# Two places instead of six for the value products of layer 1's attention, in a two-layer kernel on one core

## The chip, the cores and the metric

The kernel runs on one core of a Trainium2 chip. The engines of that core work side by side and each takes its own instructions in order: TensorE (PE, matrix products), VectorE (DVE), ScalarE (ACT), GpSimd (POOL) and SyncE (SP, which issues DMAs). The metric is the device time of one execution in microseconds (us); lower is better. Three executions before the change took 1373.52, 1379.36 and 1386.26 us; their median is 1379.36 us.

## The reference

The program is two transformer layers over x of shape (2, 1024, 256). Each adds an attention part and a feed-forward part to x, both taken from the same layer norm. The change touches only the attention of layer 1, which has 16 heads and one shared latent (64 values per token) for keys and values:

```
scores = (einsum('bhsc,btc->bhst', q_abs, kv) + einsum('bhsd,bxtd->bhst', q_pe, k_pe)) * SCALE
scores = where(causal, scores, finfo.min)
attn = softmax(scores, axis=-1)
x = einsum('bhst,btc->bhsc', attn, kv)
x = einsum('bhsc,hdc->bhsd', x, out_absorb)
return x.transpose(0, 2, 1, 3).reshape(b, s, NH * VH) @ wo.T
```

The third einsum, weights times latent, is the "value product" of the title.

## The kernel before

Layer 0 and the preparation of layer 1 (feed-forward, layer norm, latent, joined weights) come first and end some 712 us into the execution. What follows is layer 1's attention, which ends the program.

**How it is tiled.** The queries are cut into blocks of 128 tokens: two batch entries b, and in each the blocks i = 7 down to 0, the longest first. A block is worked in two halves of eight heads (g = 0, 1). One half of a block is a *step*: 32 steps, and two more turns of the loop that only drain. Block i sees the first w = 128 (i + 1) keys because of the causal mask, so a head has two score products where i is 4 or more (512 keys, and the remaining 512, 384, 256 or 128), and one where i is 3 or less.

**One head's path.** `scores` (L1165) multiplies queries with keys on PE into a PSUM bank of the tag "s", of which there are two (the pool has `bufs=2`). L1179 on DVE reads that bank, adds the mask, writes the result to SBUF as `p` and carries a running minimum `nmax` from a head's first bank to its second; the bank is then free for the next score product. L1186 on ACT takes the exponential of the whole row and its sum. Two heads later `turn_over` (L1190) on DVE transposes `p` in 32x32 blocks into `pT`. When all eight heads of a step are there, `product` (L1212) multiplies `pT` with the latent `vrep`: the call `product(s, sb)` takes 32 keys out of each quarter and issues eight small matmuls (32 rows by 64 columns of the array each, 128 columns of data), accumulated over sb = 0 .. nsb - 1 with nsb = 4 (i + 1) in the four banks `ps_o`. The profile counts two PE records for each fp32 matmul, so one sb is 16 records.

**What sets the order.** The stage is under a manual schedule: the order of the Python calls is the order on each engine. The loop at L1266 goes through the steps; in each there are nine *places*, h = 0 to 8, and at place h it issues, in this order: the score products of head h (none at place 8), then what was put on `late[h]` (work for DVE, ACT and POOL), then what was put on `side[h]` (work for PE), then one `turn_over` of the head two before. What is put where:

- `side[0]`: the rotary part of the queries of the next block (`project("pe")`, L1122, 16 records); `late[1]`: the previous step's reciprocal (`inverse`, L1193) and the rotation (`rotate`, on DVE, ACT and POOL).
- `side[1]`, only in steps with g = 1: the output projection of the block before (`output`, L1241, 16 records).
- `side[2]`: the latent part of the queries of the next block (`project("lat")`, L1122, 16 records), and behind it the first value products.
- `side[2]` to `side[7]`: the value products of the previous step.
- `side[7]`, last: `inverse_T` (L1203), which turns the reciprocals on PE (L1206, 4 records); ACT copies them (L1210), and `late[8]`, `normalize` (L1224), multiplies `ps_o` with them on DVE.

The line that deals the value products to places is the one that is changed; `prev` is the step before, and n its nsb:

```
n = prev.nsb
for sb in range(n):
    side[2 + 6 * sb // n].append(lambda sb=sb: product(prev, sb))
side[7].append(lambda: inverse_T(prev))
late[8].append(lambda: normalize(prev))
```

## Time and profile before

| what | value |
|---|---|
| three executions | 1373.52, 1379.36, 1386.26 us |
| the profiled execution, its own time | 1381.07 us |
| its span, first to last instruction | 1379.4 us |
| mean granted TensorE clock | 0.939 of full |
| busy over the span: PE, DVE, ACT, POOL | 1222.4, 823.1, 634.3, 559.8 us |
| share of the chain that ended last: PE, DVE, ACT | 67%, 13%, 7% |
| layer 1's attention | from 712 us to the end of the span |
| PE busy from 760 to 1320 us, by stretches of 40 us | 38.62 to 40.00 us each |
| DVE busy in the same stretches | 21.65 to 31.09 us each |

A row of the profile names the line, the engine, the operation, its tiles (out<-in), its shape and the number of records. In a timeline the first column is the start in us from the beginning of the span, the second the length, and a bracket at the end gives the engine's idle time before the row and what released it. Matmuls are pipelined and their ends are modelled, so the length of a PE row holds some time in which the next one already runs: the distance from one PE row's start to the next one's start is the better measure. `DVE_READ_ACCUMULATOR2_ANT` is the second half of L1179, which delivers `nmax`.

### The profile page before, as it was taken

How to read it: one execution, taken by the hardware profiler on the slowest of the kernel's cores; microseconds unless marked ns; L12 is line 12 of the kernel's file. 1: busy time of each engine (PE TensorE's matmuls, PEld its weight loads, DVE VectorE, ACT ScalarE, POOL GpSimd, SP SyncE). 2: the span in 40 equal slices, each digit the busy share in tenths (PEclk: the TensorE clock that was granted, in tenths of full speed). 3: DMA queues.
4: the chain of work that ended last, by engine and by line, in shares of the span. 5: the costliest groups of instructions: out<-in, count | busy, mean ns of one | idle time of the engine just before them, and what ended most of it. 6: DMA issues, size and time to landing. Idle time of an engine off the chain costs nothing.

```text
span 1379.4 us, 36540 instructions
## 1 busy us (share of the span) xinstructions
PE 1222.4 (89%) x15295; PEld 839.5 (61%) x15295; DVE 823.1 (60%) x2098; ACT 634.3 (46%) x1193; POOL 559.8 (41%) x644
## 2 busy tenths in 40 slices
PE   6778888887878886679778999999999999999998
PEld 3545555564545554557554667676775676777675
DVE  3775665655566416533307777776657777766653
ACT  2545656654455552223215434444555444444553
POOL 4575556554462431474214322323454232243340
PEclk9779999999998997779959999999999999999998
DMA  7463323322220003000340000000000000000000
GB/s 175 125 137 89 61 62 81 74 62 47 62 39 9 1 1 122 23 7 25 77 126 8 3 14 3 14 14 14 14 14 13 14 8 10 14 14 6 13 19 13
DMA packets 139044, 56.06 MB, mean 41 GB/s; under 512 B 110112, under 2 KB 136096, under 8 KB 138656
## 3 DMA queue, kind: packets, MB, share of 16 engines
q1 hardware_dynamic: 133296, 48.10, 14.5%
q10 hardware_dynamic: 4816, 3.02, 0.7%
q0 software_dynamic: 768, 2.62, 0.7%
q8 instruction: 120, 1.97, 0.6%
q14 instruction: 44, 0.36, 0.1%
HBM read 36.93 MB, written 14.68 MB: 37 GB/s over the span
## 4 chain that ended last, share of the span: by engine, by line
PE 67%; DVE 13%; ACT 7%; issue 4%; POOL 3%; DMA 3%; SPq 2%; ACTq 0%; DVEq 0%; POOLq 0%
PE ps_s L1173 19%; PE ps_o L1217 12%; PE ps_t L1122 7%; DVE masked L499 4%; PE ps_t L1241 4%; PE ps_o L574 4%; PE ps_m L679 3%; PE ps_ms L484 2%; PE ps_ms L537 2%; DVE p L1179 2%; PE ps_m L358 1%; ACT p L551 1%; PE ps_ms L543 1%; PE ps_o L1003 1%; PE ps_m L635 1%
## 5 line engine op out<-in xcount | busy, mean ns | idle before, releaser
L1186 ACT ACTIVATE p<-p,nmax 128x1024 f32<-128x1024 f32 (+7 forms) x256 | 198.4, 775 | 330.2 <-DVE nmax L1179 329.2
L1173 PE MATMUL ps_s<-kT,qc 128*128 128x512 f32 (+3 forms) x768 | 309.5, 515 | 7.5 <-DVE nmax L1179 7.0
L551 ACT ACTIVATE p<-ps_ms 128x1024 f32<-128x1024 f32 x144 | 147.3, 1026 | 168.5 <-PE ps_ms L543 167.5
L1191 DVE STREAM_TRANSPOSE pT<-p 128x1024 f32<-128x1024 f32 (+7 forms) x256 | 197.8, 773 | 0.2 <-ACT p L1186 0.2
L1173 PEld LDWEIGHTS ps_s<-kT,qc 128*128 128x128 f32 x768 | 127.3, 192 | 111.0 <-issue 65.2
L1217 PE MATMUL ps_o<-pT,vrep 32*64 32x128 f32 x9216 | 183.3, 281 | 1.9 <-DVE xT L1226 1.8
L1217 PEld LDWEIGHTS ps_o<-pT,vrep 32*64 32x64 f32 x9216 | 138.4, 131 | 71.2 <-issue 63.0
L1198 POOL COPY rb<-rinv 128x512 f32<-128x512 f32 x32 | 19.6, 612 | 377.0 <-DVE rinv L1196 349.2
L1140 POOL TENSOR_TENSOR qc<-t,t 32x512 f32<-32x512 f32 x128 | 161.9, 1265 | 8.2
L1179 DVE CUSTOM_DVE_ANT_0 p<-ps_s,zeros 128x512 f32<-128x512 f32 x128 | 87.6, 684 | 69.9 <-PE ps_s L1173 69.2
L1179 DVE CUSTOM_DVE_ANT_0 p<-ps_s,maskz 128x512 f32<-128x512 f32 (+3 forms) x128 | 62.2, 486 | 81.5 <-PE ps_s L1173 81.2
L492 DVE TENSOR_REDUCE peak<-ps_ms 128x2 f32<-128x1024 f32 x64 | 77.5, 1218 | 38.0 <-PE ps_ms L484 37.9
L559 POOL TENSOR_SCALAR_AFFINE_SELECT p<-p 128x256 f32<-128x256 f32 (+1 forms) x112 | 47.8, 442 | 113.1 <-ACT p L551 112.7
L537 PE MATMUL ps_ms<-head,head 64*128 64x512 f32 (+3 forms) x384 | 65.1, 377 | 25.1 <-DVE peak L499 22.2
L499 DVE CUSTOM_DVE_ANT_0 masked<-ps_ms,maskz,peak 128x512 f32<-128x512 f32 (+3 forms) x128 | 70.4, 550 | 27.0 <-PE ps_ms L484 22.3
L574 PE MATMUL ps_o<-p,v 128*32 128x512 f32 (+3 forms) x768 | 82.7, 520 | 0.0
L1179 DVE CUSTOM_DVE_ANT_0 p<-ps_s,maskz,nmax 128x512 f32<-128x512 f32 (+3 forms) x128 | 70.5, 551 | 20.2 <-PE ps_s L1173 3.6
L1136 POOL TENSOR_TENSOR t<-t,sinq 128x512 f32<-128x512 f32 x32 | 40.7, 1271 | 93.4 <-ACT t L1135 89.6
L484 PE MATMUL ps_ms<-head,head 64*128 64x512 f32 (+3 forms) x384 | 71.7, 417 | 7.1 <-DVE head L424 5.6
L652 POOL TENSOR_TENSOR h<-whole,h 128x512 fp32r<-128x512 f32 x32 | 41.0, 1280 | 87.4 <-ACT h L650 87.4
L499 DVE CUSTOM_DVE_ANT_0 masked<-ps_ms,maskz 128x512 f32<-128x512 f32 (+3 forms) x128 | 62.6, 489 | 12.2 <-PE ps_ms L484 6.5
L1122 PEld LDWEIGHTS ps_t<-qnT,wpe 96*128 96x128 f32 x512 | 63.2, 196 | 10.6 <-ACT t L1135 3.4
(239 smaller groups left out, 2095.5 us busy)
## 6 DMA issues: line engine op xcount, KB each, us to landing
stage<-rows SPq DMA_DIRECT2D x232, 64.0 KB, 2.8
rows<-proj SPq DMA_DIRECT2D x13, 512.0 KB, 3.3
rows<-proj SPq DMA_DIRECT2D x14, 256.0 KB, 2.6
v<-rows SPq DMA_DIRECT2D x32, 64.0 KB, 2.8
wo<-in_wo SPq DMA_DIRECT2D x8, 256.0 KB, 3.5
x<-x_sb SPq DMA_DIRECT2D x8, 256.0 KB, 3.2
xin<-x SPq DMA_DIRECT2D x16, 128.0 KB, 2.2
out<-xin SPq DMA_DIRECT2D x16, 128.0 KB, 1.7
```

The lines of the kernel that those rows point to most:

```text
L484: nc.tensor.matmul(t[:, c % 2, off + col : off + col + w], q[:, i * P : (i + 1) * P], k[:, k0 : k0 + w], start=True, stop=True, tile_posit ...
L499: nc.vector.tensor_tensor_reduce(masked[:, :w], at, maskz[:, SC - w :], -1.0, dst if k0 else 3.0e38, ALU.add, ALU.min, dst,)
L537: nc.tensor.matmul(t[:, c % 2, off + col : off + col + w], k[:, j * P : (j + 1) * P], q[:, at - w : at], start=(off + col == 0), stop=Fals ...
L551: nc.scalar.activation(p, t, AF.Exp)
L574: nc.tensor.matmul(quad(box["o"], c)[:, SC - w :], values[g % 2][:, j, c, :], p[:, c % 2, off + col : off + col + w], start=first, stop=fi ...
L1122: nc.tensor.matmul(box[key][:, r * P : (r + 1) * P], w[:, c, QP * g + r, :], qnT[:, c, tok], start=(c == 0), stop=(c == 1),)
L1140: nc.gpsimd.tensor_tensor(qc[b, i][64 + 32 * x : 96 + 32 * x, g, hh], t1[at : at + 32], t2[at : at + 32], ALU.add,)
L1173: nc.tensor.matmul(sc[:, : n1 - n0], qc[s.b, s.i][:, s.g, h // QP, h % QP, :], kT[:, s.b * S + n0 : s.b * S + n1], start=True, stop=True,)
L1179: nc.vector.tensor_tensor_reduce(s.p[:, n0:n1], sc[:, : n1 - n0], mask, -1.0, 3.0e38 if n0 == 0 else s.nmax, ALU.add, ALU.min, nmax,)
L1186: nc.scalar.activation(p[:, :w], p[:, :w], AF.Exp, bias=nmax, scale=-1.0, accum_out=rsum)
L1191: nc.vector.transpose(s.pT[:, : s.nsb, h, :], p[:, : 32 * s.nsb])
L1217: nc.tensor.matmul(s.o[64 * hh : 64 * hh + 64, c, : QP * 32], vrep[32 * c : 32 * c + 32, s.b * 32 + sb, :], s.pT[32 * c : 32 * c + 32, sb, ...
```

## The change

One line. The index of the place goes from `2 + 6 * sb // n` to `2 + 3 * (2 * sb // n)`:

```
                 if prev is not None:
                     n = prev.nsb
                     for sb in range(n):
-                        side[2 + 6 * sb // n].append(lambda sb=sb: product(prev, sb))
+                        side[2 + 3 * (2 * sb // n)].append(lambda sb=sb: product(prev, sb))
                     side[7].append(lambda: inverse_T(prev))
                     late[8].append(lambda: normalize(prev))
```

The first half of the sb go to place 2 and the second half to place 5; places 3, 4, 6 and 7 have none. For nsb = 32 that is two runs of 16 calls (128 matmuls, 256 records) where there were six runs of 5 or 6. For nsb = 4 there were four runs of one call, at places 2, 3, 5 and 6, and there are now two runs of two. The number of matmuls, their operands and their order among each other stay the same; DVE, ACT, POOL and SP have the same instructions in the same order.

## Prediction before the run

> **What bounds it now.** I first read busy time by step of layer 1's attention, cutting from one inverse_T to the next. The columns are length, then busy time and records of PE, its weight loads, DVE, ACT, POOL, then clock and DMA.

> ```profile
> 775.59:801.79 26.20, 26.05 (x586) 17.20 (x581) 20.27 (x44) 11.92 (x22) 6.94 (x6) 1.00 0.01 3
> 801.79:830.14 28.35, 28.35 (x537) 19.44 (x533) 20.16 (x45) 11.65 (x22) 6.94 (x6) 1.00 0.06 17
> ...
> 879.70:901.14 21.44, 20.87 (x457) 15.09 (x453) 15.99 (x44) 10.24 (x21) 6.94 (x6) 1.00 0.01 3
> ...
> 962.67:977.90 15.23, 15.23 (x316) 10.55 (x309) 10.14 (x30) 8.56 (x21) 6.95 (x6) 1.00 0.01 2
> ```

> PE is never idle for long; DVE has a quarter to a third of each step free, ACT and POOL more. So a step costs what PE's queue costs. But part of that is no arithmetic. The PE timeline, where starts count:

> ```profile
> 784.68 1.65 PE L1217 MATMUL ps_o<-pT,vrep 32*64 32x128 f32 x96
> 786.26 1.77 PE L1173 MATMUL ps_s<-kT,qc 128*128 128x512 f32 x4
> ...
> 857.52 1.46 PE L1173 MATMUL ps_s<-kT,qc 128*128 128x512 f32 x4
> 858.82 3.62 PE L1241 MATMUL ps_t<-wvo,xT 128*128 128x256 f32 x16
> ...
> 868.06 1.21 PE L1217 MATMUL ps_o<-pT,vrep 32*64 32x128 f32 x64
> 869.20 1.56 PE L1173 MATMUL ps_s<-kT,qc 128*128 128x512 f32 x4
> 870.69 1.21 PE L1217 MATMUL ps_o<-pT,vrep 32*64 32x128 f32 x64
> ```

> 96 records take 1.58 us to the next start, 64 take 1.14: 0.22 per sb (16 records), and 0.26 that doesn't grow with the run. The two scores of i = 5 (512 and 256 keys) take 1.30 ahead of other full-array work and 1.49 between two runs. So each run between scores costs 0.45 beside its arithmetic: 0.25 at its end, 0.10 on entry, and 0.10 by which the first scores behind it are slower.

> Third, all engines at the one bank wait of a step, at places 1 and 2 (i = 5, g = 0), where no run stands between two heads:

> ```profile
> 833.71 1.46 PE L1173 MATMUL ps_s<-kT,qc 128*128 128x512 f32 x4
> ...
> 834.77 0.69 DVE L1179 CUSTOM_DVE_ANT_0 p<-ps_s,zeros 128x512 f32<-128x512 f32 x1
> 835.39 0.08 DVE L1179 DVE_READ_ACCUMULATOR2_ANT nmax<- 128x1 f32 x1
> 835.52 1.56 PE L1173 MATMUL ps_s<-kT,qc 128*128 128x512 f32 x4 [0.36 <-DVE nmax L1179]
> 835.61 0.48 DVE L1179 CUSTOM_DVE_ANT_0 p<-ps_s,maskz,nmax 128x256 f32<-128x256 f32 x1
> 836.02 0.08 DVE L1179 DVE_READ_ACCUMULATOR2_ANT nmax<- 128x1 f32 x1
> ```

> A 512-key score is 0.86 (858.82 - 857.52 over 768 keys). DVE starts 0.20 after it ends; PE gets the bank back 0.75 after DVE's start; the 512 and 256 of head 1 were through at 835.0, so PE stood 0.52, and the scores behind it took 0.10 longer (1.40 to the next start, not 1.30): a restart. This is what the change will multiply.

> **Removed: run ends.** Runs of three or more sb: 0.10 going in, 0.35 coming out to scores, 0.25 to inverse_T, which follows the last run before the change. A step had 0.6 + 5 x 0.35 + 0.25 = 2.6 and keeps two runs, 0.9: 1.70 saved. Short runs cost less (32 records at 1323.48 take 0.62, so 0.18 beyond 0.44), and those steps save 1.28 (nsb 8 and 12), 0.76 (nsb 4) or 1.56 (nsb 16). By the product's own nsb: 16 x 1.70 + 4 x 1.56 + 8 x 1.28 + 3 x 0.76 = **46.0 us**. All of it is on PE, so on the path. The arithmetic stays; that a run of 16 sb keeps 0.22 per sb is extended from 4 to 6 sb.

> **Added: bank waits.** Heads 3, 4, 5 and 6, 7, 0 now stand without products between them, and only two "s" banks exist. Rows for DVE per head: 0.82 from the first pass to the second; 0.55 for a second pass of 384 keys, 0.41 of 256, 0.28 of 128; transposes 1.16 (1024 keys), 1.03, 0.89, 0.76, down to 0.23 for 128. A head's DVE order is first pass, second pass, transpose of the head two before. Worked for i = 6, from head 3's start after the run. PE 0 to 0.96 (restart in it), DVE from 1.16, bank back at 1.91; PE was through at 1.60 and stands 0.31. Head 4: 1.91 to 2.87 to 3.51. DVE: second pass 1.98 to 2.53, transpose to 3.56, then head 4's first bank, back at 4.31: PE stands 0.80. So 1.11 and two restarts, 0.20. After the second run head 7 stands 0.31 again; inverse_T (0.49) shortens the next wait to 0.31 at head 0. Then DVE, late by its wait for ACT's copy (0.85 idle before normalize), holds heads 1 and 2 too, more so where g = 0, since no output projection covers them.

> I carried the same rules through all steps, before and after, with the other rows of PE (1.79 for either query part, 3.46 for an output projection, 0.49 for inverse_T), the normalize and rotation rows of DVE, and ACT's exponentials (1.25 for 1024 keys) and copies. On before they give inverse_T distances of 26.2, 28.4, 23.8, 25.8, 21.4, 23.2, 18.0, 20.5, against 26.20, 28.35, 23.82, 25.74, 21.44, 23.19, 17.96, 20.38 measured. Bank waits more than before, g = 0 / g = 1, and restarts: i = 6: 3.14 / 2.20, ten; i = 5: 3.13 / 2.47, ten; i = 4: 3.19 / 2.88, ten; i = 7: 1.04 / 1.06, five (g = 1 alone in the first batch entry); i = 3: 0.34 / 0.09; i = 2: 0.60 / 0.18; i = 1: 0.69 / 0.26; i = 0: 0.80 / 0.67 (three restarts a pair, four for i = 0). With i = 0 at 1.03 / 0.88 / 0.29 at the end, the sum is 21.7 + 23.5 = **45.2 us**, and 94 restarts x 0.10 = **9.4 us**. i = 7 gets little because DVE bounds its pairs already and 512 keys refill the second bank; i < 4 has one bank per head, so PE runs a whole head ahead.

> Net: -46.0 + 45.2 + 9.4 = **+8.6 us**; i = 4 to 6 lose about 20, i = 0 to 3 win about 11. Nothing else moves: SP, POOL, ACT and DVE keep their order; normalize isn't nearer, as it waits for inverse_T's copy; products end earlier, nobody waits for that.

> Bounds: the 0.75, 0.20 and 0.10 are each good to about 0.03; all three off the same way, the steps worked again give +4.5 or +13. The profiled execution (span 1379.4, 1381.07 in all) lies within 2 us of the median 1379.36, so I add to the median: 1388.

> **The clock.** A trace row speaks for a further cost. At 1347.71 PE had stood 1.32 us for nmax; 32 product records then took 1.22 instead of 0.69, and the clock read 0.50 from 1350 to 1358. Against: from 735 to 750, in step 0, PE stood 0.62 to 0.71 in every 2.65 us and the clock stayed 1.00. Mine are 0.3 to 0.9; two of 0.74 with 1.17 of work between them (i = 4) come nearest to 1.3. I take nothing and keep 5 us per fall (10 us at half clock, from that row) for the range.

> [...]

> **Rivals.**
> 1. Faster: the waits are cheaper than worked. The loop from a score's end to its bank's return is 0.20 + 0.75 = 0.95. Worked again without restarts and with a loop of 0.85, the net is +0.5; with 0.66 it is -6: 1373. It decides from 0.85 down. For it: I have only one such wait in each g = 0 step, and in step 0, to read the loop from. Against: these rules give back every step of before to about 0.1 us. 0.12.
> 2. Slower: the clock falls. Five to eight falls at 5 us: 1404 to 1428. It decides from a third fall on. 0.17.
> 3. Slower: long runs don't keep 0.22 per sb, because PE's supply of weights or instructions falls behind past 48 matmuls, of which a run now has up to 128. 1 ns more per record is 9 us; 1397 and up. Against: slope equal from 48 to 96 records, so up to 48 matmuls. 0.09.
> 4. The dealing does less than said: only for nsb = 4, in the sum already.

> The forecast as worked, 1384 to 1393, has 0.62.

> **Numbers.** 1388. The range goes from 1375 (the nearer part of rival 1; the lower bound less the 6 us by which the three runs scatter is 1378) to 1403 (upper bound and two falls of the clock). About 1% (14 us) is what a measurement can tell: slower by more than that takes nearly all of rivals 2 and 3, 0.23, and 0.07 of the forecast, at its upper bound with scatter on top: 0.30. Faster by more is the extreme of rival 1 with scatter on top: 0.04. Between them 0.66.

> **What would show it.** Product rows of x256 at 3.5 to 3.8 us; inverse_T distances for i = 6, 5, 4 longer by about 1.0 to 2.0, for i = 3 to 1 shorter by 0.4 to 1.4; PE's idle for nmax at L1173 up by tens of us; clock 1.00 through i = 6 to 4. Wrong if i = 4 to 6 also shrink, if the clock falls there, or if x256 rows exceed 3.9.

## The result, and the profile after

The changed kernel took 1425.87 us (median of four, 1424.47 to 1428.13) against 1376.44 us before (median of four, 1372.6 to 1386.26). The ratio is 1.0349, 95% interval 1.029 to 1.0409: slower by 3.5%, where 1388 us and a range of 1375 to 1403 had been predicted. The profiled execution has a span of 1422.8 us, 43.4 us more than before's 1379.4.

PE's rows in the groups by line, over layer 1's attention (busy us, mean ns, then the idle time before the rows and what ended it):

```profile
L1173 PE MATMUL ps_s<-kT,qc 128*128 128x512 f32 (+3 forms) x768 | 309.0, 520 | 38.4 <-DVE nmax L1179 34.7 <-issue 0.7
L1217 PE MATMUL ps_o<-pT,vrep 32*64 32x128 f32 x9216 | 158.6, 277 | 27.9 <-issue 25.9 <-DVE xT L1226 2.0
```

The first row was foreseen: the wait of the scores for a bank (nmax) was 7.0 us and is 34.7. The second was not. In before, the value products waited for nothing but 1.8 us on `xT`; now PE stands 25.9 us in front of them on "issue", that is, with no engine and no DMA of the program to wait for. The same two rows in before:

```profile
L1173 PE MATMUL ps_s<-kT,qc 128*128 128x512 f32 (+3 forms) x768 | 309.5, 515 | 7.5 <-DVE nmax L1179 7.0
L1217 PE MATMUL ps_o<-pT,vrep 32*64 32x128 f32 x9216 | 183.3, 281 | 1.9 <-DVE xT L1226 1.8
```

Busy time by step, columns as in the prediction (i = 6 with g = 0 and 1, i = 4 with g = 0, i = 2 with g = 0), against 26.20, 28.35, 21.44 and 15.23 us before:

```profile
777.30:808.50 31.20, 26.32 (x581) 17.11 (x580) 20.05 (x44) 11.97 (x22) 6.94 (x6) 1.00 0.01 2
808.50:841.14 32.64, 28.64 (x534) 19.50 (x532) 19.95 (x45) 11.88 (x22) 6.92 (x6) 1.00 0.05 15
898.43:926.27 27.84, 23.83 (x454) 16.66 (x452) 16.05 (x45) 10.30 (x22) 6.92 (x6) 0.88 0.01 2
987.02:1001.54 14.52, 14.16 (x309) 10.54 (x308) 9.76 (x28) 8.47 (x21) 6.95 (x6) 1.00 0.01 2
```

The last step is shorter by 0.7 us, as it should be; the others are longer by 4.3 to 6.4 us, where 1 to 2 were worked out. DVE's busy time is the same to 0.4 us, and PE's to 0.3 us in the first two steps: PE does the same work with holes in it. (In the third, PE's busy time grew too, from 20.87 to 23.83 us, and the clock column reads 0.88; that comes below.) PE's timeline in the first step that has long runs shows the holes:

```profile
756.19 2.90 PE L1217 MATMUL ps_o<-pT,vrep 32*64 32x128 f32 x184
760.27 1.37 PE L1217 MATMUL ps_o<-pT,vrep 32*64 32x128 f32 x72 [1.17 <-issue]
761.56 3.97 PE L1173 MATMUL ps_s<-kT,qc 128*128 128x512 f32 x8
766.15 2.03 PE L1173 MATMUL ps_s<-kT,qc 128*128 128x512 f32 x4 [0.62 <-DVE nmax L1179]
768.11 2.71 PE L1217 MATMUL ps_o<-pT,vrep 32*64 32x128 f32 x171
772.02 1.55 PE L1217 MATMUL ps_o<-pT,vrep 32*64 32x128 f32 x85 [1.20 <-issue]
```

A run of 256 records isn't one row, as expected, but two, with a *stop* between them: after 184 records in the first run, after 171 in the second. From one stop to the next PE has done 72 value records, 12 of the six score products, and 171 to 172 value records: 256. Both runs of i = 7 need 5.4 us to the next scores; 16 x 0.222 + 0.25 = 3.80 was worked out. So a stop costs 1.6 us. That is more than the idle time in its bracket, since the rows on both sides of a hole are longer as well: 184 records took 2.90 us, where 11.5 x 0.222 is 2.55.

Doing this for every run in which the profile names a stop (distance from its start to the next other row, less 0.222 per sb and 0.25) gives 21 stops and 33.5 us: 1.12 to 2.04 each. A 22nd stop, of 0.74 us, lies at the scores. The step lengths, in us, for the first batch entry ("worked" is the length before plus the prediction's waits and restarts, less its run ends):

| i, g | before | worked | measured | stops | measured less stops |
|---|---|---|---|---|---|
| 6, 0 | 26.20 | 28.14 | 31.20 | 1.63 + 1.47 | 28.10 |
| 6, 1 | 28.35 | 29.36 | 32.64 | 1.85 + 1.37 | 29.42 |
| 5, 0 | 23.82 | 25.73 | 28.84 | 1.63 + 1.40 | 25.81 |
| 5, 1 | 25.74 | 27.03 | 28.45 | 1.35 | 27.10 |
| 4, 0 | 21.44 | 23.41 | 27.84 | 1.54 | 26.30 |
| 4, 1 | 23.19 | 24.83 | 24.95 | none | 24.95 |
| 3, 0 | 17.96 | 16.81 | 16.82 | none | 16.82 |
| 2, 0 | 15.23 | 14.47 | 14.52 | none | 14.52 |

Only one row is off by more than 0.12 us: i = 4, g = 0. There the clock fell, right behind a stop of 1.17 us that ended at 912.05. PE alone, stretches of 2 us; the column behind the number of records is the clock:

```profile
912.00:914.00 2.00, 1.65 (x6) 1.00 0.03 8
914.00:916.00 2.00, 1.73 (x2) 0.55 0.00 0
916.00:918.00 2.00, 1.64 (x4) 0.50 0.00 0
918.00:920.00 2.00, 2.00 (x20) 0.50 0.00 0
```

It cost 2.9 us (26.30 - 23.41). The second batch entry has one such fall too, at 1286, worth 2.7.

### The profile page after: what moved, and what is told of

Same layout as the page of the kernel before. It is cut to its first block, busy times and chain, and to the rows that moved or that the text cites. A ratio compares the mean times of both kernels' runs of the same rounds, so it can differ in the third digit from the quotient of the medians.

```text
span 1422.8 us, 36540 instructions
## 1 busy us (share of the span) xinstructions
PE 1206.2 (85%) x15295; PEld 838.1 (59%) x15295; DVE 812.1 (57%) x2098; ACT 631.7 (44%) x1193; POOL 559.0 (39%) x644
## 3 DMA queue, kind: packets, MB, share of 16 engines
q8 instruction: 120, 1.97, 0.6%
## 4 chain that ended last, share of the span: by engine, by line
PE 56%; DVE 19%; ACT 8%; issue 7%; POOL 4%; DMA 3%; SPq 2%; DVEq 0%; ACTq 0%; POOLq 0%
PE ps_s L1173 13%; PE ps_o L1217 11%; DVE p L1179 6%; PE ps_t L1122 6%; PE ps_t L1241 4%; DVE masked L499 4%; PE ps_o L574 3%; DVE pT L1191 3%; PE ps_m L679 3%; PE ps_ms L484 2%; PE ps_ms L537 2%; ACT p L551 2%; PE ps_m L358 1%; ACT p L1186 1%; PE ps_o L1003 1%
## 5 line engine op out<-in xcount | busy, mean ns | idle before, releaser
L1173 PE MATMUL ps_s<-kT,qc 128*128 128x512 f32 (+3 forms) x768 | 309.0, 520 | 38.4 <-DVE nmax L1179 34.7
L1173 PEld LDWEIGHTS ps_s<-kT,qc 128*128 128x128 f32 x768 | 128.4, 193 | 172.6 <-DVE nmax L1179 121.6
L1217 PE MATMUL ps_o<-pT,vrep 32*64 32x128 f32 x9216 | 158.6, 277 | 27.9 <-issue 25.9
L1217 PEld LDWEIGHTS ps_o<-pT,vrep 32*64 32x64 f32 x9216 | 137.8, 132 | 50.7 <-issue 46.2
L1179 DVE CUSTOM_DVE_ANT_0 p<-ps_s,zeros 128x512 f32<-128x512 f32 x128 | 86.1, 673 | 135.4 <-PE ps_s L1173 135.3
L1179 DVE CUSTOM_DVE_ANT_0 p<-ps_s,maskz 128x512 f32<-128x512 f32 (+3 forms) x128 | 60.1, 470 | 73.4 <-PE ps_s L1173 73.4
L1179 DVE CUSTOM_DVE_ANT_0 p<-ps_s,maskz,nmax 128x512 f32<-128x512 f32 (+3 forms) x128 | 70.5, 551 | 19.4 <-PE ps_s L1173 1.9
L499 DVE CUSTOM_DVE_ANT_0 masked<-ps_ms,maskz 128x512 f32<-128x512 f32 (+3 forms) x128 | 62.6, 489 | 11.5 <-PE ps_ms L484 5.8
```

The lines of the kernel that those rows point to most:

```text
L499: nc.vector.tensor_tensor_reduce(masked[:, :w], at, maskz[:, SC - w :], -1.0, dst if k0 else 3.0e38, ALU.add, ALU.min, dst,)
L1173: nc.tensor.matmul(sc[:, : n1 - n0], qc[s.b, s.i][:, s.g, h // QP, h % QP, :], kT[:, s.b * S + n0 : s.b * S + n1], start=True, stop=True,)
L1179: nc.vector.tensor_tensor_reduce(s.p[:, n0:n1], sc[:, : n1 - n0], mask, -1.0, 3.0e38 if n0 == 0 else s.nmax, ALU.add, ALU.min, nmax,)
L1217: nc.tensor.matmul(s.o[64 * hh : 64 * hh + 64, c, : QP * 32], vrep[32 * c : 32 * c + 32, s.b * 32 + sb, :], s.pT[32 * c : 32 * c + 32, sb, ...
```

## The experiments

Two theories stood at the start. **S**: PE's instructions arrive in blocks, and a long dense run of small matmuls uses them up faster than they come; the worked bank waits are right, and the stops are extra. **W**: the bank waits cost about twice what was worked out. A third, **R**, is a rival to both: something in a long run itself (its time on the array, PE's queue) stops it.

**low2: two places only where a step has one score product per head.**

```
low = s is not None and s.i < 4
place = 2 + 3 * (2 * sb // n) if low else 2 + 6 * sb // n
side[place].append(lambda sb=sb: product(prev, sb))
```

> Two places only in the steps whose own block has i < 4; six places where i is 4 or more. Theory S (PE's instruction supply stops in long runs, about 1.5 us each, on top of the bank waits as I worked them): no run here is longer than 10 sb, so no stop; the worked net is -11 us, 1365 with before at 1376. Rival W (the bank waits cost about twice what I worked, and make the 46 us): the waits of these steps are 7.6 us in all, doubled 15, net -4, 1372. Both: the steps of i = 7 to 4 keep their length of before.

Measured: 1365.93 against 1380.77 us, ratio 0.9879 (0.9835 to 0.9922), so 17 us less by the ratio and 15 by the medians. There was one stop, 1.7 us, in a run of 10 sb:

```profile
L1217 PE MATMUL ps_o<-pT,vrep 32*64 32x128 f32 x9216 | 167.9, 277 | 3.4 <-DVE xT L1226 2.0 <-issue 1.3
```

Steps of i = 3 to 1 were as short as in the changed kernel (18.98, 14.52, 16.47, 12.00 us, for example), those of i = 7 to 4 as long as before. So the saving on run ends is real, and the short end of the change was a gain. It came out larger than the 11 us worked; 3.5 us of that lie in the last block (i = 0), in which before had its clock at 0.50 for 10 us from 1350 us on.

**three: three places, runs of at most 176 records.**

```
side[2 + 2 * (3 * sb // n)].append(lambda sb=sb: product(prev, sb))
```

> Three places (2, 4, 6), runs of at most 11 sb (176 records). Worked net without any stop -2.5 us. Theory S: stops of PE on issue become few, as most came after more than 170 records of a run: 1374 to 1382. Rival W (bank waits doubled, 24 us more): about 1398. Rival R (runs of more than 6 sb are slow in themselves): x176 rows well above 2.7 us, some 1395.

Measured: 1384.11 against 1380.77 us, ratio 1.0017 (0.9995 to 1.0038); 6 stops with 6.9 us of idle time:

```profile
L1217 PE MATMUL ps_o<-pT,vrep 32*64 32x128 f32 x9216 | 160.4, 275 | 8.9 <-issue 6.9 <-DVE xT L1226 1.8
```

That is S: 2 to 3 us above before, where S allowed 2 below to 6 above, and W and R asked for some 20 above. Runs of 176 records without a stop lasted 2.70 us (one of them 3.08), which is 11 x 0.222 + 0.25 to 0.01.

**few: long runs with a quarter of the instructions.** Every second `product` call returns at once, so half of the keys are left out; the others do this:

```
if sb % 2:
    return
for c in range(4):
    nc.tensor.matmul(
        s.o[0:64, c, : 2 * QP * 32], vrep[32 * c : 32 * c + 32, s.b * 32 + sb, :],
        s.pT[32 * c : 32 * c + 32, sb, :, :],
        start=(sb == 0), stop=(sb == s.nsb - 2), tile_position=(32 * c, 0),
    )
if sb == 0:
    ...
```

> The places as changed (2 and 5), but every second value product is left out, and the others take all eight heads at once (256 columns instead of two times 128): a run keeps PE busy for nearly as long (8 x 0.44 instead of 16 x 0.22 us) with a quarter of the matmul and weight-load instructions. The output is not the attention's, since half of the keys are left out. Theory S: no stop on issue at the value products; worked net with the longer first product +15 us against before: 1391. Rival R (the length of a run in time is what stops PE): the stops stay, about 1425. Rival W: 1425 or more, without stops.

Measured: 1384.21 against 1380.77 us (one execution). PE's timeline in a step of i = 6:

```profile
792.79 3.42 PE L1218 MATMUL ps_o<-pT,vrep 32*64 32x256 f32 x60
796.14 3.69 PE L1173 MATMUL ps_s<-kT,qc 128*128 128x512 f32 x8
800.44 1.77 PE L1173 MATMUL ps_s<-kT,qc 128*128 128x512 f32 x4 [0.61 <-DVE nmax L1179]
802.14 3.68 PE L1218 MATMUL ps_o<-pT,vrep 32*64 32x256 f32 x64
805.75 3.69 PE L1173 MATMUL ps_s<-kT,qc 128*128 128x512 f32 x8
```

Runs of 3.6 us, and no stop on issue at the value products in the whole trace. The bank waits are all there; the row of the scores and the row of the products in this kernel:

```profile
L1173 PE MATMUL ps_s<-kT,qc 128*128 128x512 f32 (+3 forms) x768 | 304.6, 514 | 37.9 <-DVE nmax L1179 35.0
L1218 PE MATMUL ps_o<-pT,vrep 32*64 32x256 f32 x2304 | 139.7, 381 | 3.1 <-DVE pT L1191 3.1
```

35.0 us for nmax against 34.7 in the changed kernel: the same waits, without the loss. W with twice the waits would need 1425, and R as far as it goes by time on the array would need the stops; both are out. Steps of i = 6 to 4 took 27.73, 29.05, 25.44, 26.77, 23.19 and 24.64 us, under the 28.14 to 24.83 worked for the changed kernel by 0.2 to 0.4: a run here, 3.61 us (792.52 to 796.14 and 802.14 to 805.75), is shorter than the 3.80 of a full one and the 4.02 that I had taken for the first, which is one part of why the total is under my 1391. The miss is larger than that: this run is 3 us above before, where 15 had been worked out, and from its first scores on the stage took 653.8 us (before 657.1). Part of the rest is the short steps and the last block, which gained more than worked; I have not split it up further. The clock stayed at 1.00 in all of these steps. And the DMA queue list shows what the instructions are carried in. The queue of this kind in the changed kernel, and then in few (packets, MB, share):

```profile
q8 instruction: 120, 1.97, 0.6%
```

```profile
q8 instruction: 68, 1.11, 0.3%
```

The edit took 9216 - 2304 - 256 = 6656 matmul records away and as many weight loads, 13,312 instructions; the queue has 52 packets less, and 13,312 / 52 = 256. A packet is 1.97 MB / 120 = 16.4 KB. So one packet holds a block of 256 instructions of PE in these runs, or 128 value records with their weight loads.

**one4: all value products in one run at place 4.**

```
side[4].append(lambda sb=sb: product(prev, sb))
```

> All value products of a step in one run at place 4, up to 32 sb (512 records). Worked net without stops -4 us: 1372. Theory S: one stop of about 1.5 us for every 256 records beyond the first 170 or so, 2 each in i = 7, 6, 5 and 1 each in i = 4, 3, some 32 stops: 1415 to 1425. Rival W: bank waits doubled (46 more): 1418, with no stops at the value products.

Measured: 1439.76 against 1380.77 us (one execution), where S had said 1415 to 1425 with some 32 stops; 40 stops at the value products, 53.0 us of idle time. PE's timeline for a run of 512 records:

```profile
1112.48 3.41 PE L1217 MATMUL ps_o<-pT,vrep 32*64 32x128 f32 x223
1117.17 2.08 PE L1217 MATMUL ps_o<-pT,vrep 32*64 32x128 f32 x128 [1.28 <-issue]
1120.64 2.08 PE L1217 MATMUL ps_o<-pT,vrep 32*64 32x128 f32 x128 [1.39 <-issue]
1124.11 0.76 PE L1217 MATMUL ps_o<-pT,vrep 32*64 32x128 f32 x33 [1.39 <-issue]
```

I had expected a stop for every 256 records; it is every 128. This is the rate itself: 128 records (256 instructions) every 3.47 us (1117.17 to 1120.64), while PE needs 8 x 0.222 = 1.78 for them. Over the whole trace there are 20 such distances, 3.45 to 4.01 us, with a median of 3.47. The first 223 are what was at hand: the rest of a block, 95, and a whole one.

The trace also holds the times of the instruction packets. Here they lie at 1114.72 to 1115.60, 1118.29 to 1119.30 and 1121.77 to 1122.69 us. PE goes on 1.57, 1.34 and 1.42 us after each has ended, and the next one starts 1.12 or 1.13 us after PE has gone on. In the changed kernel too, all 22 stops end 1.2 to 1.6 us after the end of such a packet. So what PE waits for at these stops is the next block.

This gives S a sharper form: a block takes about 3.4 us to come (an estimate from the times above: 1.12 to the start of a packet, 1.01 for it and 1.34 until PE goes on make 3.47) and is ordered when a block is used up (no row shows the order; it is inferred from those 1.12 and 1.13 us), so a run stops only if it meets a second block edge within that time. In a run of 128 records that should hardly happen; all eight runs of 256 in the changed kernel did stop.

**runs8: four places, runs of at most 128 records; best: what the sums favoured.**

```
side[(3, 4, 6, 7)[4 * sb // n]].append(lambda sb=sb: product(prev, sb))
```

> Four places (3, 4, 6, 7), so runs of 8 sb at most: 128 records, as many as one block of 256 instructions holds. Theory S in its sharper form (PE's instructions come in blocks of 256, a block takes about 3.4 us to come and is ordered when a block is used up, so a run stops only if it crosses two block edges within that time): no stop at all; worked net without stops -16 us, ratio 0.988. Rival W (bank waits cost twice what is worked): some 0 us. Rival R' (every run of more than 100 records stops once): about 8 runs of 128, 112 or 96 records a step, 12 to 20 us more than worked.

```
low = s is not None and s.i < 4
place = 4 + 2 * (2 * sb // n) if low else 3 + 5 * sb // n
side[place].append(lambda sb=sb: product(prev, sb))
```

> Five places (3 to 7, runs of at most 7 sb) in steps whose own block has i of 4 or more, two places (4 and 6) where i is below 4. Worked net without stops -26 us: ratio 0.981, some 1354. Theory S: at most one or two stops, in the runs of 10 sb behind i = 4. Rival W: about -24, since few bank waits are left: this run doesn't tell W apart, it is the version that should beat both kernels.

Measured: runs8 1362.32 against 1381.83 us, ratio 0.9868 (0.9827 to 0.9909), and no stop that the profile names (five of its runs are 0.1 to 0.3 us longer than worked, 1.0 us together). best 1354.44 against 1381.83 us, ratio 0.9802 (0.9769 to 0.9836), with two stops, 1.4 us. One of them, 0.29 us, lies behind record 62 of a run of only 96; the record 128 places before it started 3.62 us earlier, in the run before. So what counts is how soon one block edge follows another, not the length of one run. Its rows of scores and value products, the same view as after the change:

```profile
L1173 PE MATMUL ps_s<-kT,qc 128*128 128x512 f32 (+3 forms) x768 | 298.3, 505 | 8.2 <-DVE nmax L1179 7.3
L1217 PE MATMUL ps_o<-pT,vrep 32*64 32x128 f32 x9216 | 163.2, 276 | 3.3 <-DVE xT L1226 1.8 <-issue 1.4
```

Both idle times are back near those of before, with fewer run ends. This version beats both kernels: before by 2.0% (1.6 to 2.3%), and the changed one by some 5%, if the times of the two sets of runs may be compared.

**shift32: the blocks moved against the program.** `for f in pe_ * (3 if g == 0 else 1): f()` ahead of the first step puts 64 instructions in front of the steps.

> The changed kernel with 16 matmuls (32 records with 32 weight loads, 64 instructions) put in ahead of the first step: the first query projection is computed three times, the last one is used. Nothing in the steps changes. Theory S (block edges of 256 instructions): every stop comes 32 records earlier in its run. In the changed kernel the first two runs of i = 7 stopped after 184 and 171 records, the next two after 242 and 230; here after 152 and 139, 210 and 198. Rival R'' (the place of a stop depends on the run, on PE's queue or on DVE): the stops stay after 184, 171, 242, 230. The time itself: some 7 us more than 1426 under both, since PE is at half clock there and 32 records take 7 us.

PE's rows at the value products of the same four runs:

```profile
762.24 2.46 PE L1217 MATMUL ps_o<-pT,vrep 32*64 32x128 f32 x152
765.97 1.81 PE L1217 MATMUL ps_o<-pT,vrep 32*64 32x128 f32 x104 [1.26 <-issue]
...
774.25 2.27 PE L1217 MATMUL ps_o<-pT,vrep 32*64 32x128 f32 x139
776.69 1.98 PE L1217 MATMUL ps_o<-pT,vrep 32*64 32x128 f32 x117 [0.17 <-issue]
...
793.38 3.27 PE L1217 MATMUL ps_o<-pT,vrep 32*64 32x128 f32 x210
798.06 0.96 PE L1217 MATMUL ps_o<-pT,vrep 32*64 32x128 f32 x46 [1.42 <-issue]
...
804.96 3.10 PE L1217 MATMUL ps_o<-pT,vrep 32*64 32x128 f32 x198
809.68 1.15 PE L1217 MATMUL ps_o<-pT,vrep 32*64 32x128 f32 x58 [1.63 <-issue]
```

152, 139 (where the stop was only 0.17 us), 210 and 198: all four where S puts them. The rival is out. One run of 256 records (1133.64) had no stop: it lasted 3.8 us, and its second edge fell among the scores behind it, which stood 0.21 us on issue. The total was a miss: 1415.58 against 1381.57 us (one execution each), 10 us under the changed kernel instead of 7 over. From the first scores on, the stage took 686.9 us against 701.9 in the changed kernel. With the edges elsewhere there were 17 stops with 18.5 us, not 21 with 25.9, and no fall of the clock in i = 4.

## Why the prediction was wrong

- **What bounds the kernel** was right: PE's queue, and the run ends in it.
- **Removed: run ends** was right. Steps without long runs are shorter by what was worked out, to 0.1 us (16.82 for 16.81, 14.52 for 14.47), and low2 is faster by 1.2%.
- **Added: bank waits and restarts** was right. The step lengths in the table, less their stops, agree to 0.12 us except where the clock fell, and few shows the same waits alone. (In the second batch entry one step is 0.2 us over, and one 1.1, the one with the stop at the scores.) The profile names only 34.7 - 7.0 = 27.7 us as more idle time for nmax, not 45.2: a PE row's end hides part of a wait, as where the prediction worked 0.52 us and the bracket says 0.36. An estimate from that difference is 94 x 0.16 = 15 us hidden, 43 in all.
- **The step that failed** is a sentence in "Removed": "that a run of 16 sb keeps 0.22 per sb is extended from 4 to 6 sb". The slope held (a run of 14 sb without a stop lasted 3.36 us, 14 x 0.222 + 0.25), but not the flow. The danger was named as rival 3, "PE's supply of weights or instructions falls behind past 48 matmuls", and given 0.09, on the evidence of a slope from 48 to 96 records. All of those runs were shorter than one block of 128, so they could not have shown it, and the price was put as a slower slope instead of a stop of 1.6 us. The sum put the stops at nothing; 21 of them took 33.5 us.
- **The clock**: I took nothing, and two falls of 2.9 and 2.7 us came. Both followed a stop, and few, with the same bank waits and no stops, kept 1.00 through i = 6 to 4. So the waits of 0.3 to 0.9 us alone didn't do it, as argued; the stops, which the sum lacked, came before both (1.17 and 1.60 us). That is a pairing in these traces, not shown by a run made for it, and a stop alone is not enough: in shift32 none of 17 was followed by a fall, and in one4 only two of 40, both of 1.92 us, while a third of 1.92 us left the clock at 1.00. What else decides stays open.

The sum as it should have been, against the profile's +43.4: +8.6 as worked, +33.5 for stops, +0.7 for one at the scores (the 0.7 us on issue in the L1173 row), +5.6 for the clock, -3.7 in the last block (i = 0: 9.30 and 7.93 us for 11.05 and 9.86), -1.4 because the stage began earlier (first scores at 720.84, before at 722.23): 43.3. That it meets the profile to 0.1 us is partly luck: the last block's figure is taken against before, not against its worked length, and it holds a clock that read 0.50 for 10.2 us in before (1349.7 to 1359.9) and for 3.4 here (1395.5 to 1398.9).

The blocks could have been suspected from the page of before. It lists 120 instruction packets with 1.97 MB, as the changed kernel's does, and 15,295 matmul and as many weight-load records of PE; 30,590 / 120 is 255 a packet. A run of 256 records with its loads is two such packets in 3.6 us, while a step of before used 586 records in 26.2 us, a packet every 5.7 us. The block of 256 is what few and one4 show (13,312 instructions in 52 packets; 128 records every 3.47 us). The profile names no stop at the value products in before, with a packet every 5.7 us in that step, and none in runs8; in the changed kernel (21 stops) and in one4 (40) PE had used up what was at hand before the next block came.

## What to carry to other kernels

A dense run of small matmuls had a length here that the instruction supply could feed: one4 got 256 PE instructions (128 fp32 records with their loads) every 3.45 to 4.01 us, with up to one more block at hand (223 records before the first stop of the run shown above). Grouping this work saved the ends of runs, 0.45 us each, until a second block edge came too soon behind the first; from there on the changed kernel lost some 1.6 us per stop (33.5 us for 21). And where, as here, the other engine has only two banks to take from PE, keep a run of something between the heads (PE's idle time for nmax was 34.7 us in the changed kernel and 7.3 in best): the best version put runs of 7 sb at each of five places where heads have two score products, and two runs of 10 or less where they have one.
